# Halo attention and a factored convolution on one core: in layer 0, when the row loads are issued, where the top rows' transfers stand, how the norm's steps are spread, and what is loaded first

## The chip, the core and the metric

The kernel runs on one core of a Trainium2 chip. A core has five engines with an instruction stream each: PE (matrix products), DVE (vector), ACT (scalar functions), POOL and SP, and 16 DMA engines that move data between the memories. In this kernel SP does nothing but issue transfers, in the order in which they are written; one that has to wait holds up all behind it. The metric is the time on the device in microseconds (us), over several runs. Everything is in 32-bit floating point.

## The reference, cut to what matters

The input `x` is two images of 128 channels by 256 by 256.

```python
# layer 0: group norm, attention inside windows of 8 x 8 pixels, residual
x = x + attention(gn(x))
#   q, k, v = W_qkv applied to each pixel; 4 heads of 32
#   a window's 64 queries see the 12 x 12 pixels around it, less those that FIXED_MASK strikes out
#   logits = q k + relative position (row, column) + FIXED_MASK; softmax; times v; W_out
# layer 1: group norm, a vertical convolution of 5 taps and one of 3, times a mix of 8 groups; residual
x = x + conv(gn(x))
```

Group norm needs the mean and the variance of the whole image (4 channels to a group) before any pixel of it can be normalised: `gn` of image 0 stands ahead of all attention. The mask leaves, for each query, 6 x 6 of the 12 x 12 keys, so that even and odd pixel rows fall apart into separate problems.

## The kernel before, in words

Layer 0 is `attention_fast`. Its first part, the setup, loads all of image 0 in 32 pieces of 8 rows (`f_sx`, 1 MB each, L266), and DVE takes their statistics two rows at a time with `bn_stats` (L128). The constants (`f_wqkvT`, `f_hot` and others) are loaded ahead of these pieces by `cload` (L201) and L244, L246. `load_rows(0)` and `load_rows(1)` come last and bring the first two strips for the attention itself.

The attention then goes through 64 strips `k` (32 to an image, 8 new rows each), and each strip in two units `u = 2k` and `u = 2k + 1` (even and odd pixel rows), 128 units in all. All engines' orders, SP's too, are those of the written code (`manual_schedule(engines=ORDERED)`). A unit is, on PE: `biases` (L565), `scores` (L582), the next unit's `keys` (L385, `f_pk`), the next strip's `coefficients` (L476, `f_pa`), `attend` (L608, `f_o`), then in an even unit the next strip's `values` (L498, `f_pv`), in an odd one two units' `queries` (L448, L450), and last `project` (L385, `f_py`). `PIECES` sets into how many matmuls some of these are cut. ACT takes the exponentials (L592), four in a unit, as the scores come; DVE the reciprocals of the softmax's sums (L614), three in a unit.

What SP issues in layer 0, by name:

- `load_rows(k + 2)`, at the start of an even unit: the 10 rows of a later strip into one of three `f_raw` buffers, in five transfers of two rows (L319). DVE normalises them in `normalise(k + 2)` at the start of the odd unit (L359), the first thing that it does there.
- `load_next()`, right after it, in image 0 alone: up to 10 rows of image 1 for its statistics, into the one buffer `f_sx`, also by twos (L306). `input_stats` reads them at the start of the next even unit.
- `bring(r, ...)`: the values from `f_vn` to where the windows need them, `f_vt`, in 6 or 12 transfers (L528, L532, L535), for `r = 0` after `values` of the even unit, for `r = 1` after `attend` of the odd unit, whose reads of `f_vt1` it has to wait for.
- `bring_top(r, b)`: 12 small transfers (L545, L549, L552) of an image's first two rows from `f_top`, a tile that shares the buffer of `f_sx`. `bring_top(1, 0)` stands ahead of unit 0, `bring_top(1, 1)` at the end of unit 63, after that unit's `bring(1, ...)`.
- the store of the unit's result (L646), at the unit's end, waiting for DVE's `project` (L642).

Between the statistics and a usable mean stand six steps (`Norms.steps`): a matmul, a row of short DVE instructions, a matmul, a DVE instruction, a square root on ACT, and DVE again. Unit 60 takes all six for image 1's input, unit 70 all six for image 0's result, at fixed places called `step()`.

Layer 1, `convolutions_fast`, follows at about 1906 us.

## Time and profile before

| | |
|---|---|
| runs, median (lowest to highest) | 2912.95 us (2910.43 to 2917.16) |
| the profiled execution's own time | 2912.66 us |
| its span on the core | 2910.7 us |
| PE busy / DVE / ACT / POOL | 95% / 73% / 52% / 22% of the span |
| granted PE clock, mean | 0.997 |
| setup, until the first unit | 113.2 us |
| units 0 and 1 | 32.8 us |
| units 2 to 59 (image 0) | 814.2 us |
| units 60 to 65 (from image 0 to image 1) | 93.0 us |
| units 66 to 127 (image 1) | 853.2 us |
| the rest (layer 1) | 1004.3 us |

A unit begins with the first matmul of L565, so the lengths of the units are the distances between these in the timeline. In the profile, a row of the waits names the engine and line that waited, what ended the wait, the total, how often, and the longest. A row of the timeline gives start, length, engine, line, operation, tiles, how many such instructions are merged in it, and in brackets the idle time before it and what ended it; "issue" stands where the profile shows nothing that the engine waited for.

### The profile page before, as it was taken

How to read it: one execution, taken by the hardware profiler on the slowest of the kernel's cores; microseconds unless marked ns; L12 is line 12 of the kernel's file. 1: busy time of each engine (PE TensorE's matmuls, PEld its weight loads, DVE VectorE, ACT ScalarE, POOL GpSimd, SP SyncE). 2: the span in 40 equal slices, each digit the busy share in tenths (PEclk: the TensorE clock that was granted, in tenths of full speed). 3: DMA queues.
4: the chain of work that ended last, by engine and by line, in shares of the span. 5: the costliest groups of instructions: out<-in, count | busy, mean ns of one | idle time of the engine just before them, and what ended most of it. 6: DMA issues, size and time to landing. Idle time of an engine off the chain costs nothing.

```text
span 2910.7 us, 117791 instructions
## 1 busy us (share of the span) xinstructions
PE 2766.5 (95%) x51762; PEld 2095.5 (72%) x51762; DVE 2134.0 (73%) x3601; ACT 1506.9 (52%) x2379; POOL 643.1 (22%) x2049
## 2 busy tenths in 40 slices
PE   0699999999999999999999999999999999999998
PEld 0489899899989888999998999954444444444444
DVE  8567667676666656555565665579999998999987
ACT  0345454454545545454544545456666666666654
POOL 1233333333333333333323333200000000000000
PEclk9999999999999999999999999999999999999999
DMA  9666666666666455555555555557888887888885
GB/s 394 208 187 173 189 174 179 181 160 188 175 162 164 125 146 126 138 141 136 140 126 137 138 138 140 129 142 210 221 220 214 216 218 213 222 212 212 221 217 146
DMA packets 207528, 521.89 MB, mean 179 GB/s; under 512 B 26304, under 2 KB 103584, under 8 KB 178336
## 3 DMA queue, kind: packets, MB, share of 16 engines
q1 hardware_dynamic: 197936, 448.19, 53.1%
q0 software_dynamic: 9072, 66.06, 12.2%
q8 instruction: 412, 6.75, 1.0%
q14 instruction: 108, 0.88, 0.1%
HBM read 284.78 MB, written 134.22 MB: 144 GB/s over the span
## 4 chain that ended last, share of the span: by engine, by line
PE 77%; issue 18%; POOL 1%; DVE 1%; SPq 1%; DMA 1%; ACT 1%; POOLq 0%; DVEq 0%; ACTq 0%
PE f_s L582 9%; PE f_o L608 8%; PE f_pk L385 8%; PE f_pv L498 8%; PE f_py L385 8%; PE a_o L890 6%; PE a_e L890 6%; PE f_pq L450 6%; PE f_pa L476 5%; PE f_s L565 5%; PE f_pq L448 2%; PE a_d L941 2%; PE a_c L890 1%; PE b L983 1%; PE g L870 1%
## 5 line engine op out<-in xcount | busy, mean ns | idle before, releaser
L489 DVE TENSOR_SCALAR f_cf<-f_pa,f_keep 128x512 f32<-128x512 f32 x128 | 103.7, 810 | 534.4 <-ACT f_cf L485 534.3
L592 ACT ACTIVATE f_p<-f_s 128x512 f32<-128x512 f32 x512 | 264.4, 602 | 419.9 <-PE f_s L582 419.9
L456 ACT ACTIVATE f_q<-f_pq,f_head 128x512 f32<-128x512 f32 x512 | 303.6, 703 | 150.3 <-PE f_pq L450 150.3
L399 POOL COPY f_kt<-f_kt 128x60 f32<-128x60 f32 (+1 forms) x348 | 106.2, 341 | 1202.4 <-ACT f_kt L413 1178.6
L376 POOL COPY f_xq<-f_xn 128x96 f32<-128x96 f32 x1024 | 337.2, 362 | 9.9 <-DVE f_xn L359 9.9
L965 ACT ACTIVATE t<-t,w 128x1024 f32<-128x1024 f32 x127 | 145.9, 1148 | 368.6 <-DVE t L958 363.7
L972 DVE SCALAR_TENSOR_TENSOR t<-t,w,t 128x1024 f32<-128x1024 f32 x254 | 325.9, 1283 | 7.4 <-ACT t L965 1.3
L582 PEld LDWEIGHTS f_s<-f_q,f_kt 64*64 64x64 f32 x17176 | 270.3, 132 | 49.2 <-issue 49.2
L582 PE MATMUL f_s<-f_q,f_kt 64*64 64x64 f32 (+1 forms) x17176 | 287.8, 220 | 0.0
L608 PE MATMUL f_o<-f_vt,f_p 128*32 128x66 f32 x16384 | 269.6, 220 | 14.2 <-issue 14.1
L608 PEld LDWEIGHTS f_o<-f_vt,f_p 128*32 128x32 f32 x16384 | 244.3, 108 | 27.2 <-issue 18.0
L498 PE MATMUL f_pv<-f_wqkvT,f_xn 128*128 128x128 f32 x2048 | 251.0, 279 | 10.9 <-issue 9.4
L385 PE MATMUL f_pk<-f_xn,f_wqkvT 128*128 128x192 f32 (+3 forms) x1496 | 257.9, 322 | 0.7 <-ACT f_kt L413 0.7
L1001 POOL DMA_DIRECT2D y<-f_x x63 | 54.7, 868 | 918.7 <-DVE y L993 871.3
L498 PEld LDWEIGHTS f_pv<-f_wqkvT,f_xn 128*128 128x128 f32 x2048 | 235.4, 192 | 20.2 <-issue 13.4
L385 PE MATMUL f_py<-f_ot,f_woT 128*128 128x160 f32 (+1 forms) x1520 | 245.9, 311 | 3.0 <-DVE f_ot L626 1.8
L890 PE MATMUL a_o<-xm,w1s 128*128 128x512 f32 x512 | 242.2, 594 | 4.4 <-ACT t L881 4.4
L890 PE MATMUL a_e<-xm,w1s 128*128 128x512 f32 x512 | 240.7, 591 | 0.0
L385 PEld LDWEIGHTS f_py<-f_ot,f_woT 128*128 128x128 f32 x1520 | 228.9, 191 | 5.4 <-issue 2.2
L385 PEld LDWEIGHTS f_pk<-f_xn,f_wqkvT 128*128 128x128 f32 x1496 | 221.4, 190 | 12.6 <-issue 1.7
L450 PE MATMUL f_pq<-f_xn,f_wq_s 128*128 128x192 f32 (+1 forms) x1008 | 210.2, 331 | 0.0
L615 DVE TENSOR_TENSOR f_on<-f_o,f_rc 128x320 f32<-128x320 f32 (+1 forms) x384 | 197.1, 513 | 13.3
(149 smaller groups left out, 4663.2 us busy)
## 6 DMA issues: line engine op xcount, KB each, us to landing
f_raw<-in_x SPq DMA_DIRECT2D x308, 256.0 KB
f_x<-f_x SPq DMA_DIRECT2D x128, 512.0 KB
y<-f_x POOLq DMA_DIRECT2D x63, 1024.0 KB, 7.8
out<-y SPq DMA_DIRECT2D x63, 1024.0 KB
f_vt<-f_vn SPq DMA_DIRECT2D x172, 264.0 KB
raw<-f_x SPq DMA_DIRECT2D x64, 640.0 KB
f_sx<-in_x SPq DMA_DIRECT2D x32, 1024.0 KB
f_sx<-in_x SPq DMA_DIRECT2D x128, 256.0 KB
```

Of the source, the lines that this page charges most:

```text
L376: nc.gpsimd.tensor_copy(xq[:, half, t2, 1:4, :, c].rearrange("p t r n e -> p r t n e"), xn[k % 2][:, windows, :, c, 0:3, t2:8:4].rearrange ...
L385: nc.tensor.matmul(dst[:, 512 * lo // last : 512 * hi // last], w, moving[:, n * lo // last : n * hi // last], start=True, stop=True,)
L450: nc.tensor.matmul(by_pair[:, lo:hi, 8:32], wq_s, xn[k % 2][:, lo:hi, r, c, 0:3].rearrange("p n i j -> p n (i j)"), start=True, stop=True,)
L456: nc.scalar.activation(q[:, c, :, i].rearrange("p n (j t) -> p n j t", t=4), pq.rearrange("p (n t j) -> p n j t", n=NPAIR, t=4), AF.Copy, ...
L498: nc.tensor.matmul(pv[:, P * n : P * n + P], xn[k % 2][:, 4 * g + n].rearrange("p r c i j -> p (r c i j)"), wvT, start=True, stop=True,)
L582: nc.tensor.matmul(sc[g][n // 8][64 * c : 64 * c + 64, n % 8, lo:hi].rearrange("p i x -> p (i x)"), kt[r][rows, c, NKEY * n : NKEY * n + 6 ...
L592: nc.scalar.activation(pts[u][:, g, 8 * half : 8 * half + 8].rearrange("p n i x -> p (n i x)"), sc[g][half].rearrange("p n i x -> p (n i x ...
L608: nc.tensor.matmul(po[32 * h : 32 * h + 32, n - lo], p[:, h // 2, n, h % 2], vt[r][:, :, n, h], start=True, stop=True,)
L615: nc.vector.tensor_tensor(on[:, :, lo:hi].rearrange("p c n d -> p n c d"), po[:, :, :, 0:32], rc.to_broadcast([P, hi - lo, 2, 32]), ALU.mult,)
L890: nc.tensor.matmul(pa[:, : n * W], w, rows, start=i == 0, stop=i == len(terms) - 1)
L965: nc.scalar.activation(t3[:, j : j + 4], t1[:, j : j + 4, :], AF.Copy, scale=w3[:, 0:1])
L972: nc.vector.scalar_tensor_tensor(t3[:, j : j + 4], t1[:, j + tap : j + tap + 4, :], w3[:, tap : tap + 1], t3[:, j : j + 4], ALU.mult, ALU.add,
```

## The change

- `load_rows` is one transfer of 10 rows. It moves from the start of the even unit to after `scores`, and waits for the first exponential of the same unit (`after(...)` adds a dependence on an instruction).
- `load_next` is one transfer too. It moves to after `attend`, and waits for the unit's first reciprocal.
- `bring_top(1, b)` moves behind the `load_rows` of an image's first unit (units 0 and 64).
- The norm's steps go through a queue `chains`: two places in a unit, four in those of strips `NS - 2`. Image 1's input norm starts in unit 59; image 0's result norm starts in unit 70 as before and takes three units.
- In the setup, three pieces of `f_sx` are issued ahead of the constants, the first of them by twos. The pieces begin at row 16; the first 16 rows come with `load_rows(0)` and `load_rows(1)`, which stand at the end of the pieces and serve both the statistics and the attention.

No arithmetic is added or removed.

```diff
+        def load_rows(k, behind=None):
+            b, s = divmod(k, NS)
+            t = rawp.tile([P, 10, W], F32, tag="raw", name=f"f_raw_{k}")
+            n = min(10, H - 8 * s)
+            load = nc.sync.dma_start(t[:, 0:n, :], x[b, :, 8 * s : 8 * s + n, :])
+            if behind:
+                after(load, behind)
+            raws[k] = t
...
+            for i in range(first):
+                t = sp.tile([P, 8, W], F32, tag="sx", name=f"f_sx_0_{i}")
+                for lo in range(0, 8, 8 if i else 2):
+                    hi = lo + (8 if i else 2)
+                    nc.sync.dma_start(t[:, lo:hi], x[0, :, 8 * (i + 2) + lo : 8 * (i + 2) + hi, :])
+                ahead.append(t)
+            for t, src in constants:
+                nc.sync.dma_start(t, src)
...
+            for i in range(first, NS - 2):
+                t = sp.tile([P, 8, W], F32, tag="sx", name=f"f_sx_0_{i}")
+                nc.sync.dma_start(t, x[0, :, 8 * (i + 2) : 8 * (i + 2) + 8, :])
+                statistics(i, t)
+            for i in range(2):
+                load_rows(i)
+                statistics(NS - 2 + i, raws[i][:, 0:8])
...
-            norm_at[2 * (b * NS + NS - 2)] = st_x, b + 1, f"x{b + 1}"
-            norm_at[2 * ((b + 1) * NS + 3)] = st_y, b, f"y{b}"
+            last = 2 * (b * NS + NS - 2)
+            norm_at[last - 1] = st_x, b + 1, f"x{b + 1}"
+            norm_at[last + 10] = st_y, b, f"y{b}"
...
-                for lo in range(0, n, 2):
-                    nc.sync.dma_start(t[:, lo : lo + 2], x[b, :, row + lo : row + lo + 2, :])
+                after(nc.sync.dma_start(sxs[u], x[b, :, row : row + n, :]), seen["output"])
...
-            m = n if k < 2 else 2
-            for lo in range(0, n, m):
-                nc.sync.dma_start(t[:, lo : lo + m], x[b, :, 8 * s + lo : 8 * s + lo + m, :])
...
-                if r == 0:
-                    if k + 2 < NB * NS:
-                        load_rows(k + 2)
-                elif k + 2 < NB * NS:
+                if r == 1 and k + 2 < NB * NS:
                     normalise(k + 2)
...
-                if u == 0 or u in stats_at:
-                    load_next()
...
                 scores(u, pieces(u)[3])
-                step()
+                if r == 0:
+                    if k + 2 < NB * NS:
+                        load_rows(k + 2, seen["exp", 0, 0])
+                    if s == 0:
+                        bring_top(1, b)
                 step()
...
                     emit(keys(u + 1, cuts, cuts))
                 step()
-                step()
...
-                step()
+                if k % NS == NS - 2:
+                    step()
                 attend(u)
+                if u == 0 or u in stats_at:
+                    load_next()
                 if more and r == 1:
                     bring(1, slots_of(k + 1))
-                    if at_top:
-                        bring_top(1, b + 1)
...
                 turn(u)
-                step()
+                if k % NS == NS - 2:
+                    step()
```

## The prediction, made before the changed kernel was run

> **What bounds the kernel now.** I read the page first, then the waits, then the timeline of PE unit by unit. Page and waits:
>
> ```profile
> PE 2766.5 (95%) x51762; PEld 2095.5 (72%) x51762; DVE 2134.0 (73%) x3601; ACT 1506.9 (52%) x2379; POOL 643.1 (22%) x2049
> ...
> q8 instruction: 412, 6.75, 1.0%
> ...
> PE f_o L608 <- issue: 14.1, 23, 1.5
> ...
> DVE f_xn L359 <- DMA f_raw<-in_x: 11.5, 2, 6.2
> ...
> PE f_pv L498 <- issue: 9.4, 17, 1.4
> ```
>
> PE is the bound, and hardly waits for an engine. What it waits for is called "issue": nothing that the profile shows. The timeline of PE says where. Unit 78, and unit 80 with the same work:
>
> ```profile
> 1227.98 0.67 PE L608 MATMUL f_o<-f_vt,f_p 128*32 128x66 f32 x32
> 1229.41 1.59 PE L608 MATMUL f_o<-f_vt,f_p 128*32 128x66 f32 x96 [0.76 <-issue]
> 1230.92 3.84 PE L498 MATMUL f_pv<-f_wqkvT,f_xn 128*128 128x128 f32 x32
> ...
> 1256.33 2.05 PE L608 MATMUL f_o<-f_vt,f_p 128*32 128x66 f32 x128
> 1258.30 3.84 PE L498 MATMUL f_pv<-f_wqkvT,f_xn 128*128 128x128 f32 x32
> ```
>
> Unit 80 takes 13.67 us, unit 78 takes 14.65, and the whole difference is in f_o. From the starts of all units: 59 of the 62 odd ones from 3 to 125 take 13.7 to 13.9, so 13.7 is what PE's work needs. Even units run over it: units 2 to 58 by 19.2 us together (mostly inside f_pv), units 66 to 124 without 70 by 13.3 (nearly all inside f_o). Sum 32.5 us.
>
> Its cause is in the packet records. Queue 8 moves 412 packets of 16,384 bytes; PE has 103,524 matmul and weight-load instructions, 251 to a packet, so these are PE's own program. All long gaps end 1.2 to 1.6 us after such a packet. Three come in a unit. The first of an even unit starts at +4.1 to +4.3 us in units that lose nothing and at +4.9 to +5.5 in those that lose 0.65 to 1.3 in f_o; the second starts at about +8 in image 1, but at +9 to +10 in image 0, where f_pv is late. What holds them is in the same records: the store's 1 KB packets fill the DMA engines from +2.0 to +4.0, the row load's 2 KB packets from +4.0 to +7.6, and in image 0 the load for the statistics makes that +12.5.
>
> Two larger losses stand alone:
>
> ```profile
> 1033.08 0.59 SPq L646 DMA_DIRECT2D f_x<-f_x  x1
> 1033.71 3.07 SPq L319 DMA_DIRECT2D f_raw<-in_x  x5
> ...
> 1043.45 1.92 DVE L359 TENSOR_SCALAR f_xn<-f_raw,mean_x,rstd_x 128x512 f32<-128x512 f32 x4 [5.35 <-DMA f_raw<-in_x]
> ...
> 1046.15 0.69 PE L448 MATMUL f_pq<-f_xn,f_wq_s 128*128 128x128 f32 x2 [3.99 <-DVE f_cf L489]
> ```
>
> Unit 64's row load leaves SP only after unit 65 has begun (1033.06), behind 24 transfers, 12 of them bring_top's; DVE waits for it and PE for DVE. Unit 65 takes 20.2 us; after its gap some query matmuls take 1.49 us where 0.82 is usual (the granted clock of that stretch is 0.97). Unit 1 has the same at its row load (128.3): 17.2 us.
>
> **The change part by part.**
>
> *Row load moved and joined (even units).* Removes four of five issues. The first exponential of a unit ends at +3.0 (1252.56 + 0.60 in unit 80, begun at 1250.14). The row load then issues at +3.05; packets have followed an issue by 1.2 to 1.4 us, so they start at +4.4, after the first program packet's +4.1, where now they are queued right behind the store. Two 10-row loads stand in this trace (the setup's last): 10,240-byte packets of 0.39 us, eight to an engine, 3.1 us; it is over at about +7.5, when the second program packet is due, and lands near +8.5, over 5 us before the odd unit's normalise. Behind the waiting issue SP holds only the statistics load, bring(0) and the store, due at +8, +14 and +18: none is late. POOL issues no transfer in layer 0.
>
> *Statistics load moved.* The first reciprocal ends at +8.1 (unit 16: 352.34 + 0.22 against 344.47), so its packets run from about +9.4 to +12.5, after the second program packet and ahead of bring(0) at +13.9. Its buffer is read 14 us later. The third program packet (+12.4) has until the odd unit's +2.3.
>
> Worth together: at most the 32.5 us. I take 28.5, seven eighths, as the store still holds the first packet at times.
>
> Here a rule speaks against the change. The Trainium skill, "DMA: Bandwidth & Descriptors", section "Queues, rings and completion order": a DMA engine takes turns between queues by whole packets, about 9 to 17 descriptors, before it switches. What the trace counts as packets would be its descriptors, and the eight of a load go in one turn: 0.76 us as it is (8 x 0.095), 3.1 as changed. The delays seen now, 0.8 in image 1, fit it. So if a program packet falls behind the new load, it pays four times as much; the gain rests on the place of the load, not on its form.
>
> Another rule says there is nothing to gain: "Runtime: NRT & Kernel Launch", section "Instruction fetch mechanics", has the program stream in by 16 KiB blocks and the crossing of one mostly hidden. By it this part is worth 0. Unit 78 beside unit 80 says otherwise, 0.98 us in one unit. I go by the row.
>
> *bring_top behind the row load, units 0 and 64.* Unit 64's load leaves about 8 us earlier (12 issues of 0.62 to 0.67), near 1025.6, and lands near 1031, before unit 65 wants it. bring_top's 12 then end near 1034, 5 us before attend(65) (1039.4); unit 63's store, 8 us earlier too, frees DVE's 3.5 us wait. Unit 65 falls from 20.2 to 13.9 or so: 6.2 (between 4 and 6.5, all of its excess). Unit 1 has 3.5 to give. But the statistics load of unit 0 uses bring_top's buffer and waits for its last landing, and can then hold a program packet in unit 1: 2.5 (between 0.5 and 3.5).
>
> *Norm steps.* Unit 70 takes 16.5; f_pk there takes 3.7 us for 1.9 because both steps stand before it and ACT's copies come late. Spread, the two matmuls' 0.5 stay, and the square root brings its two table loads (1.28 us each) right after unit 72's exponentials, with some 1.5 us of slack ahead of f_o. I take 1.8 (between 0 and 2.8), and 0.3 in unit 60.
>
> *Setup.* DVE's statistics run without a gap from the first landing:
>
> ```profile
> 4.49 54.01 SPq L266 DMA_DIRECT2D f_sx<-in_x  x25
> ...
> 9.54 19.90 DVE L128 BATCH_NORM_STATS2 f_st_x<-f_sx 128x6 f32<-128x512 f32 x32 [9.54 <-DMA f_sx<-in_x]
> ```
>
> The first two rows, issued at 1.2, land near 3.9 (f_wqkvT took 2.5): 5.6 us earlier. But the DMA engines are full there (422 GB/s, 2.5 us for 1 MB) and DVE needs 2.45: it starves for 1.9 us ahead of the second piece and 1.5 ahead of the fourth, which the constants (0.55 MB, 1.4 us) delay, and 0.7 is lost on the first piece by twos and at the joins. Two loads fewer do not help DVE, which still takes 128 statistics of 0.61. Worth 1.4 (between 0 and 3).
>
> Sum against the profiled execution: 28.5 + 6.2 + 2.5 + 1.8 + 0.3 + 1.4 = 40.7. 2912.7 - 40.7 = 2872.0; that execution is within 0.3 us of the median of the runs. Layer 1's orders are not touched.
>
> **The rivals.**
>
> *Only the single losses go.* PE's program packets stay late, behind the store and the values' transfers (SBUF packets of 0.8 us), and the gaps move but stay. For it: the first packet has only 0.05 to 0.2 us to spare even in good units (+4.3, and f_o is hit from about +4.35). Against: good units have the store in front too. 2912.7 - 12.2 = 2900.5.
>
> *A program packet falls behind the joined load.* Slower. In two of three even units the first program packet starts at +4.1 or later, and the load's packets come at +4.4. If the load gets in first, the packet waits up to 3.1 us more and f_o with it. There are 62 loads, some 41 in such units: 41 x 3.1 = 127 more. With the 12.2 of the rest, 2912.7 + 127 - 12 = 3028 at worst, about 2945 where it hits a third of them. It decides from the point where 13 units (40.7 / 3.1) are hit. Against it: the exponential sets the load by PE's own progress, so the distance holds from unit to unit.
>
> *Nothing happens:* the waits of PE have another cause and the two late loads become other waits (unit 65 now for bring_top, unit 1 for the statistics load). 2910 to 2915.
>
> **How the numbers follow.** All parts as summed: 0.68, time 2872, own range 2860 to 2887. Only the single losses, or these with up to half of the gaps: 0.15, 2887 to 2904. Slower by the joined load: 0.11. Nothing: 0.06, partly on either side. What can be told from no change is 0.2%, 5.8 us. Faster 0.84, within it 0.05, slower 0.11. The range runs from 2859 to 2903, which leaves out the slow cases and little else.
>
> **What would show it.** In the profile after: even units at 13.7 to 13.9 in the timeline; the rows "PE f_o L608 <- issue" and "PE f_pv L498 <- issue" of 14.1 and 9.4 down to a few us; "DVE f_xn <- DMA f_raw" (11.5) nearly gone; units 65 and 1 near 14; unit 70 near 14; DVE's first statistics at about 4 us and its last some 1.4 us earlier than 91.1; program packets at +4.1 and +8. Wrong if f_o or f_pv rows with "issue" gaps of 2 to 3 us appear (the joined load got in front), if bring_top shows up as what attend(65) waits for, or if f_xn waits for f_raw in every odd unit.

## The result, and the profile after

The changed kernel takes 2878.03 us (median of 4 runs, 2876.19 to 2879.55), beside 2914.32 us for the kernel before on the same chip (2910.43 to 2917.16). The ratio is 0.9876, with a 95% interval from 0.9859 to 0.9893: it is 1.2% faster. The forecast was 2872.0 with a range from 2859 to 2903. The profiled execution has a span of 2875.9 us, 34.8 less than before.

The page of the changed kernel, the lines of PE and of the queue that carries its program:

```profile
PE 2753.5 (96%) x51762; PEld 2090.1 (73%) x51762; DVE 2134.2 (74%) x3601; ACT 1506.2 (52%) x2379; POOL 640.4 (22%) x2049
...
q8 instruction: 412, 6.75, 0.9%
```

The instructions and the program packets are the same in number. The waits of PE in the changed kernel (engine, line, what ended the wait: total us, times, longest), where L634 is now `attend` and L524 `values`:

```profile
PE f_pq L474 <- issue: 4.9, 1, 4.9
...
PE f_o L634 <- issue: 3.4, 3, 1.7
...
PE f_pv L524 <- issue: 0.3, 1, 0.3
```

The two rows that stood at 14.1 and 9.4 us are down to 3.4 and 0.3. The row of `f_pq` is now the largest inside the units, one wait of 4.9 us. Before, it was one wait too, and in unit 1 as well:

```profile
PE f_pq L448 <- issue: 1.9, 1, 1.9
...
142.51 0.38 PE L448 MATMUL f_pq<-f_xn,f_wq_s 128*128 128x128 f32 x1 [1.88 <-issue]
```

Unit 78 in the timeline of PE, which had lost 0.98 us in `f_o`, and the first line of unit 79:

```profile
1201.53 1.12 PE L591 MATMUL f_s<-f_cf,f_hot 32*64 32x256 f32 x32
...
1207.73 2.05 PE L634 MATMUL f_o<-f_vt,f_p 128*32 128x66 f32 x128
1209.70 3.84 PE L524 MATMUL f_pv<-f_wqkvT,f_xn 128*128 128x128 f32 x32
...
1215.21 1.12 PE L591 MATMUL f_s<-f_cf,f_hot 32*64 32x256 f32 x32
```

`f_o` is in one piece, and the unit takes 13.68 us. Unit by unit, from the first matmul of `biases` in each:

| stretch | before | after | difference | predicted |
|---|---|---|---|---|
| setup, until unit 0 | 113.2 | 115.1 | +1.9 | -1.4 |
| unit 0 | 15.6 | 15.8 | +0.2 | 0 |
| unit 1 | 17.2 | 21.0 | +3.8 | -2.5 |
| even units 2 to 58, over 13.7 each | 19.2 | 0.2 | -19.0 | } |
| even units 66 to 124 without 70 and 72, over 13.7 each | 13.3 | -0.1 | -13.4 | } -28.5 |
| unit 65 | 20.2 | 14.0 | -6.2 | -6.2 |
| units 70 and 72 | 30.2 | 29.8 | -0.4 | -1.8 |
| all else (unit 126 -1.4, layer 1 -0.5, unit 60 -0.1) | | | -1.7 | -0.3 |

In all -34.8. "Layer 1" begins here, as in the table before, with the first matmul of unit 127, whose work runs into that of layer 1 (so "units 66 to 127" there are units 66 to 126). Unit 126 and layer 1 differ as much between two executions of one kernel: layer 1 took 1003.8 us in this profile of the changed kernel and 1006.3 in a second one, unit 126 12.9 and 15.2.

The program packets, from the packet records: the first of an even unit now starts at +4.1 us (median; latest +4.4 in all 59 units), where in units 66 to 124 before 16 of 30 had started later than +4.4. The second starts at +8.0 in image 0 (before +9.3) and at +8.1 in image 1 (before +8.7).

Unit 65, on SP's queue, on DVE and on PE. SP's queue:

```profile
1012.89 0.57 SPq L253 DMA_DIRECT2D f_raw<-in_x  x1
1013.51 0.94 SPq L571 DMA_DIRECT2D f_vt<-f_top  x1
...
1017.92 0.62 SPq L571 DMA_DIRECT2D f_vt<-f_top  x1
1021.63 0.63 SPq L575 DMA_DIRECT2D f_vt<-f_top  x1
```

DVE:

```profile
1020.67 1.29 DVE L670 TENSOR_TENSOR f_x<-f_py,f_raw 128x512 f32<-128x512 f32 x2
1021.88 1.92 DVE L385 TENSOR_SCALAR f_xn<-f_raw,mean_x,rstd_x 128x512 f32<-128x512 f32 x4
```

The row load leaves SP in the middle of unit 64 (which began at 1005.67), ahead of the twelve transfers of `bring_top`, and DVE normalises right after its own work, with no wait for the load. The 5.35 us of DVE and the 3.99 of PE are gone.

Unit 1 went the other way. SP's queue, and PE:

```profile
122.32 0.39 SPq L253 DMA_DIRECT2D f_raw<-in_x  x1
...
127.67 0.62 SPq L571 DMA_DIRECT2D f_vt<-f_top  x1
131.75 0.63 SPq L575 DMA_DIRECT2D f_vt<-f_top  x1
...
134.41 0.61 SPq L578 DMA_DIRECT2D f_vt<-f_top  x1
136.67 0.33 SPq L342 DMA_DIRECT2D f_sx<-in_x  x1
```

```profile
140.97 0.27 PE L474 MATMUL f_pq<-f_xn,f_wq_s 128*128 128x128 f32 x1
146.10 0.58 PE L474 MATMUL f_pq<-f_xn,f_wq_s 128*128 128x128 f32 x1 [4.86 <-issue]
146.48 1.49 PE L476 MATMUL f_pq<-f_xn,f_wq_s 128*128 128x384 f32 x2
```

Unit 0's statistics load (L342) uses the buffer out of which `bring_top` reads, and leaves SP only at 136.67, when unit 1 (from 130.99) is 5.7 us old. Its packets run from 137.6 on, `bring`'s are right behind them, and the next program packet starts at 143.3. PE stands for 4.86 us until it has come, and its next matmuls take 1.49 us for 0.81: the granted clock is 0.50 for 6.83 us from 144.06 on.

### The profile page after: what moved, and what is told of

Read it like the earlier page. It is cut to its first block, busy times and chain, and to the rows that moved or that the text cites. A ratio compares the mean times of both kernels' runs of the same rounds, so it can differ in the third digit from the quotient of the medians.

```text
span 2875.9 us, 117447 instructions
## 1 busy us (share of the span) xinstructions
PE 2753.5 (96%) x51762; PEld 2090.1 (73%) x51762; DVE 2134.2 (74%) x3601; ACT 1506.2 (52%) x2379; POOL 640.4 (22%) x2049
## 3 DMA queue, kind: packets, MB, share of 16 engines
q0 software_dynamic: 9072, 66.06, 12.3%
## 4 chain that ended last, share of the span: by engine, by line
PE 79%; issue 17%; POOL 1%; DMA 1%; ACT 1%; DVE 1%; SPq 0%; POOLq 0%; ACTq 0%; DVEq 0%
PE f_s L608 10%; PE f_o L634 9%; PE f_pk L411 8%; PE f_pv L524 8%; PE f_py L411 8%; PE a_o L919 6%; PE a_e L919 6%; PE f_pq L476 6%; PE f_pa L502 5%; PE f_s L591 5%; PE f_pq L474 2%; PE a_d L970 2%; PE a_c L919 1%; PE b L1012 1%; PE g L899 1%
## 5 line engine op out<-in xcount | busy, mean ns | idle before, releaser
L634 PE MATMUL f_o<-f_vt,f_p 128*32 128x66 f32 x16384 | 263.6, 220 | 3.4 <-issue 3.4
L634 PEld LDWEIGHTS f_o<-f_vt,f_p 128*32 128x32 f32 x16384 | 241.8, 108 | 12.9 <-issue 2.0
L524 PE MATMUL f_pv<-f_wqkvT,f_xn 128*128 128x128 f32 x2048 | 246.0, 279 | 0.6 <-DVE f_cf L515 0.3
L524 PEld LDWEIGHTS f_pv<-f_wqkvT,f_xn 128*128 128x128 f32 x2048 | 233.7, 192 | 6.7 <-DVE f_cf L515 0.5
L411 PEld LDWEIGHTS f_pk<-f_xn,f_wqkvT 128*128 128x128 f32 x1496 | 221.5, 190 | 12.5 <-issue 1.7
L643 DVE TENSOR_TENSOR f_on<-f_o,f_rc 128x320 f32<-128x320 f32 (+1 forms) x384 | 197.2, 514 | 13.3
```

What stands on the lines that cost most here:

```text
L411: nc.tensor.matmul(dst[:, 512 * lo // last : 512 * hi // last], w, moving[:, n * lo // last : n * hi // last], start=True, stop=True,)
L524: nc.tensor.matmul(pv[:, P * n : P * n + P], xn[k % 2][:, 4 * g + n].rearrange("p r c i j -> p (r c i j)"), wvT, start=True, stop=True,)
L634: nc.tensor.matmul(po[32 * h : 32 * h + 32, n - lo], p[:, h // 2, n, h % 2], vt[r][:, :, n, h], start=True, stop=True,)
L643: nc.vector.tensor_tensor(on[:, :, lo:hi].rearrange("p c n d -> p n c d"), po[:, :, :, 0:32], rc.to_broadcast([P, hi - lo, 2, 32]), ALU.mult,)
```

## The experiments

Each was timed beside the kernel before on its chip; that kernel's median was between 2915.7 and 2920.2 us in these sets. Lengths of stretches are from the profiled execution of each. This table is the frame for what follows:

| kernel | ratio to before (95%) | setup | units 0, 1 | even 2 to 58 over 13.7 | even 66 to 124 over 13.7 (without 70, 72) | unit 65 |
|---|---|---|---|---|---|---|
| before | 1 | 113.2 | 15.6, 17.2 | 19.2 | 13.3 | 20.2 |
| after | 0.9876 (0.9859 to 0.9893) | 115.1 | 15.8, 21.0 | 0.2 | -0.1 | 14.0 |
| e1 place only | 0.9881 (0.9862 to 0.9901) | 113.7 | 15.9, 15.9 | 6.6 | 0.1 | 14.1 |
| e2 form only | 1.0046 (1.0032 to 1.0060) | 113.1 | 15.6, 17.9 | 34.1 | 14.6 | 20.0 |
| e3 no wait | 1.0025 (1.0016 to 1.0033) | 115.2 | 15.8, 19.9 | 38.6 | 10.3 | 13.7 |
| e4 old setup | 0.9848 (0.9829 to 0.9868) | 113.7 | 16.1, 17.8 | 1.1 | -0.4 | 14.0 |
| e5 statistics behind rows | 0.9996 (0.9987 to 1.0005) | 114.9 | 15.6, 16.9 | 38.5 | -0.4 | 14.6 |
| e7 unit 1 | 0.9867 (0.9846 to 0.9889) | 115.0 | 16.1, 18.1 | 1.0 | -0.4 | 14.0 |
| e8 before, shifted | 1.0794 (1.0766 to 1.0821) | 112.5 | 14.4, 16.4 | 89.9 | 101.7 | 18.2 |
| e9 after, shifted | 1.0938 (1.0890 to 1.0986) | 114.3 | 14.4, 14.5 | 128.0 | 111.5 | 15.1 |
| b1 | 0.9854 (0.9828 to 0.9879) | 113.7 | 16.1, 13.6 | 5.0 | -0.2 | 14.0 |
| b2 | 0.9856 (0.9833 to 0.9880) | 114.3 | 15.9, 13.9 | 4.3 | -0.3 | 14.0 |
| b3 | 0.9862 (0.9845 to 0.9878) | 112.8 | 15.9, 16.4 | 1.3 | 0.6 | 14.3 |

### Place, form and wait of the two loads (e1, e2, e3)

The change does three things to the two loads at once: it puts them later among SP's issues, makes one transfer of five, and lets them wait. The first run keeps place and wait and takes the form back:

```diff
-            load = nc.sync.dma_start(t[:, 0:n, :], x[b, :, 8 * s : 8 * s + n, :])
-            if behind:
-                after(load, behind)
+            m = 2 if behind else n
+            for lo in range(0, n, m):
+                load = nc.sync.dma_start(t[:, lo : lo + m], x[b, :, 8 * s + lo : 8 * s + lo + m, :])
+                if behind and lo == 0:
+                    after(load, behind)
...
-                after(nc.sync.dma_start(sxs[u], x[b, :, row : row + n, :]), seen["output"])
+                for lo in range(0, n, 2):
+                    load = nc.sync.dma_start(t[:, lo : lo + 2], x[b, :, row + lo : row + lo + 2, :])
+                    if lo == 0:
+                        after(load, seen["output"])
```

> The changed kernel with its row loads and statistics loads cut into pieces of two rows again; they stay where the change put them, the first piece behind the exponential or the reciprocal. Theory 'place' (the gain comes from the load's packets coming after the program packet): the same gain, 2875 to 2884 us, even units at 13.7 to 13.8. Theory 'form' (few large packets are handled better, or fewer issues of SP count): most of the 31 us in the even units is lost, 2900 to 2912. Theory 'size of a turn' (a packet of 2 KB yields sooner than one of 10 KB): a little faster than the changed kernel, by up to 5 us, most of it in unit 1.

Measured: 2884.38 us, ratio 0.9881, just above the range that I had expected of "place". Image 1 has the whole gain with the old form (0.1 us over). Image 0 has two thirds of it (6.6 over, and odd units 4.1 over, where the changed kernel has 0.8). PE's waits, with `values` at L529:

```profile
PE f_pv L529 <- issue: 3.7, 9, 0.7
```

The row load in pieces is over later (its last packet ends at +9.3 in the median of image 1, where nothing follows it, instead of +8.7), and the second program packet comes at +8.9 (median) instead of +8.0 in image 0 and +8.1 in image 1. It is as late in image 1, where this costs nothing. What differs is the place where PE needs the packet. Before the change PE stops in `f_pv` after 24 to 29 of its 32 matmuls in image 0, and in `f_o` after 31 to 37 of its 128 in image 1. Units 6 and 50 stop in both, 127 matmuls apart; by that distance the second place lies at the end of `f_pv` or behind it in image 1, where the packet is needed later. This is read from the traces and was not tested. In six odd units of image 0 the third packet of the unit before starts only after they have begun, and these make most of the 4.1. Unit 1 loses less here, 15.9 for 21.0, which pays half of that back. Place and wait make the gain; the form is worth some 10 us in image 0 beside it.

The second run has the form alone, in the kernel before:

```diff
-                for lo in range(0, n, 2):
-                    nc.sync.dma_start(t[:, lo : lo + 2], x[b, :, row + lo : row + lo + 2, :])
+                nc.sync.dma_start(sxs[u], x[b, :, row : row + n, :])
...
-            m = n if k < 2 else 2
-            for lo in range(0, n, m):
-                nc.sync.dma_start(t[:, lo : lo + m], x[b, :, 8 * s + lo : 8 * s + lo + m, :])
+            nc.sync.dma_start(t[:, 0:n, :], x[b, :, 8 * s : 8 * s + n, :])
```

> The kernel before with its row loads and statistics loads each joined to one transfer, at the old place and behind nothing. Theory 'place', with the rule of turns by whole packets: a program packet that falls behind a joined load waits up to 3.1 us instead of 0.76, in about 40 of the 62 even units, so up to 90 us slower, 2945 to 3010. Theory 'form': about as fast as the changed kernel in the even units, 2880 to 2890. If joining matters neither way: 2908 to 2918.

Measured: 2931.46 us, ratio 1.0046, between the ranges that I had expected. PE's waits in that kernel, with `values` at L495 and `attend` at L605:

```profile
PE f_pv L495 <- issue: 26.1, 28, 1.6
PE f_o L605 <- issue: 21.8, 22, 4.6
```

So the joined load at the old place is a loss, but one of 15 us in image 0 (34.1 for 19.2) and 1.3 in image 1, not of 90. The longest single wait of 4.6 is one case. In image 1, where the row load stands alone, as many first program packets are late as before (16 of 30 after +4.4), and the latest starts at +5.7, before +5.5. The charge of 3.1 us for a packet behind a joined load, which was estimated from the rule of turns, is not seen: image 0's second packet comes at +10.1 (before +9.3).

The third run leaves the changed kernel as it is but for the two waits:

```diff
             load = nc.sync.dma_start(t[:, 0:n, :], x[b, :, 8 * s : 8 * s + n, :])
-            if behind:
-                after(load, behind)
...
-                after(nc.sync.dma_start(sxs[u], x[b, :, row : row + n, :]), seen["output"])
+                nc.sync.dma_start(sxs[u], x[b, :, row : row + n, :])
```

> The changed kernel without its two waits: both loads stay one transfer and stay where they are written among SP's issues, but nothing holds them until the exponential or the reciprocal. Theory 'place': the row load then issues right behind the store, as before, and its packets come ahead of the first program packet; the gain of the even units is gone, 2905 or slower (slower still by the rule of turns, to 2990). If the order of SP's issues alone does it: 2875 to 2885.

Measured: 2926.64 us, ratio 1.0025. PE's waits, with `values` at L522 and `attend` at L632:

```profile
PE f_pv L522 <- issue: 27.5, 27, 1.7
PE f_o L632 <- issue: 15.8, 19, 2.3
```

The even units lose 38.6 and 10.3 us, about as with the joined form at the old place (34.1 and 14.6), and of the large gains only unit 65's stays (13.7). SP runs ahead of the unit: without the wait it issues the row load at +1.6 (median) instead of +3.0, and the statistics load at +3.4 instead of +8.1. The place in the written order decides little without the wait.

### Each load for itself (e5)

The statistics load, right behind the row load, with no wait of its own (that of unit 0 stays as it is; `u` in the first part is the unit that reads the load, 2 for unit 0's):

```diff
-                after(nc.sync.dma_start(sxs[u], x[b, :, row : row + n, :]), seen["output"])
+                load = nc.sync.dma_start(sxs[u], x[b, :, row : row + n, :])
+                if u == 2:
+                    after(load, seen["output"])
...
                 if r == 0:
                     if k + 2 < NB * NS:
                         load_rows(k + 2, seen["exp", 0, 0])
+                    if u in stats_at:
+                        load_next()
...
-                if u == 0 or u in stats_at:
+                if u == 0:
                     load_next()
```

> The changed kernel, but the statistics loads of units 2 to 58 are issued right behind the unit's row load and wait for nothing of their own (unit 0's still waits for the reciprocal). Theory 'place, for each load': their packets now run from about +7.5 to +10.6 us of the unit, on top of the second program packet (due at +8), which then comes at about +10, as in the kernel before with joined loads; f_pv in units 2 to 58 loses some 1 us each, 20 to 30 us in all, 2898 to 2908, and units 66 to 126, which have no such load, stay as in the changed kernel. If the row load's wait alone made the gain: 2876 to 2882.

Measured: 2914.41 us, ratio 0.9996. PE's waits, with `values` at L526:

```profile
PE f_pv L526 <- issue: 32.9, 28, 1.8
```

Image 1 keeps its gain (-0.4). Image 0 is 38.5 us over, 32.9 of it in the waits of `f_pv`: the second program packet comes at +10.2. These 38.5 are 8.5 above the upper end of what I expected (20 to 30), and the time is above its range: the second packet is now late in nearly every unit (28 waits), where `f_pv` had 17 before. So the row load's wait by itself is worth the 13.4 us of image 1, and in image 0 it takes both waits to win the 19.0.

### Is it the program? A shift by half a packet (e8, e9)

Thirty-two more matmuls in the setup, on data that are there, in time in which PE idles. Their results are overwritten by the same values, and nothing else is touched. The profile counts 64 more PE matmuls and 64 more weight loads: 128 instructions, half of the 251 of a packet.

```diff
-                nc.tensor.matmul(
-                    pg[:, : 2 * NREL], wq_nat[32 * h : 32 * h + 32, :],
-                    relT[32 * h : 32 * h + 32, :], start=True, stop=True,
-                )
+                for _ in range(9):
+                    nc.tensor.matmul(
+                        pg[:, : 2 * NREL], wq_nat[32 * h : 32 * h + 32, :],
+                        relT[32 * h : 32 * h + 32, :], start=True, stop=True,
+                    )
```

> The kernel before with 32 extra matmuls in the setup (in time that PE is idle), 128 PE instructions, half of a program packet; all else is untouched. If the gaps of the even units are PE's program coming late, they must leave their places: the three crossings of a unit lie about 2.3 us earlier (near +0, +4.4 and +9.3 instead of +2.3, +6.6 and +11.6), so f_o and the end of f_pv no longer show gaps and other lines do; the sum can be larger or smaller, 2900 to 2940. If the gaps belong to the lines or to an engine's late result: same rows f_o and f_pv 'issue', 2912 to 2922.

> The changed kernel with the same 32 extra matmuls. The new places of the loads were read against where the program packets stand now. If the gain depends on that: the packets come about 2.3 us earlier in the unit, into the store's transfer (+2 to +4) and into the row load (+4.4 to +7.5), and the even units lose again, 2890 to 2930. If any spacing of the loads does it: 2876 to 2884.

Measured: 3147.45 us for the kernel before with the shift, 1.0794 of the kernel before, and 3199.1 us for the changed kernel with the shift, 1.0938. Both are far outside all that I had expected. PE's waits in the kernel before with the shift (`attend` at L609):

```profile
PE f_o L609 <- issue: 182.2, 110, 4.3
```

And its unit 80 in the timeline of PE:

```profile
1394.83 1.62 PE L609 MATMUL f_o<-f_vt,f_p 128*32 128x66 f32 x97
1398.96 0.66 PE L609 MATMUL f_o<-f_vt,f_p 128*32 128x66 f32 x31 [2.50 <-issue]
1399.56 5.47 PE L499 MATMUL f_pv<-f_wqkvT,f_xn 128*128 128x128 f32 x32
```

The waits of `f_pv` are gone, and `f_o` stops instead, 110 times in the 128 units and up to 4.3 us, in unit 80 after 97 of its 128 matmuls (`f_pk` stops 28 times, for 17.0 us). How far the stop has moved can be read in unit 78, which before stopped after 32 matmuls of `f_o`:

```profile
1361.98 1.59 PE L609 MATMUL f_o<-f_vt,f_p 128*32 128x66 f32 x96
1365.81 1.11 PE L609 MATMUL f_o<-f_vt,f_p 128*32 128x66 f32 x32 [2.25 <-issue]
```

The stop stands 64 matmuls with their 64 weight loads away from there, as many instructions as were added; the same holds in units 66, 110 and 122 (after 31, 36 and 37 before, after 95, 100 and 101 here). Packet records of unit 80: program packets at +1.9, +7.9 and +12.3; the row load's packets start at +3.7 and nine tenths of them are over by +7.4, the last at +10.4. PE goes on at +10.3, 1.4 us after the second packet has come (7.93 + 0.93). In the odd units, which have no row load, the second packet starts at +6.2 (median of image 1). Against these, the even ones have it 1.7 us later (median +7.87 for +6.18) with the row load in pieces of 2 KB, and 1.95 us later (+8.15 for +6.20) as one transfer of 10-KB packets in the changed kernel with the shift. After such a gap the values can be slower too: 5.47 us for 3.84. The changed kernel with the shift has the same row, larger:

```profile
PE f_o L635 <- issue: 214.7, 111, 6.8
```

128 instructions that no engine waits for move the time by 231 us in one kernel and by 321 in the other. Of the 231, from unit 0 to unit 127, 168 are idle time of PE (204 us for 36) and 62 are slower matmuls; the granted clock stands at 0.50 in 23 stretches of 3.41 us there. Nothing but the place of the program's blocks has changed, against the transfers and against the matmuls. That settles what PE waits for under the name "issue". What makes a packet late is not settled as far: the odd units, in which neither of the two loads runs, lose 64 us too with the shift (35.2 in image 0 and 28.3 in image 1), and what delays their packets was not looked into. The pair also says that the change is good for one alignment: with the shift the changed kernel is the slower of the two by 1.6% (3199.1 against 3147.45, same chip).

### The setup (e4, and the late constants in b2)

The changed kernel with the setup of before:

```diff
-            for i, t in enumerate(ahead):
-                statistics(i, t)
-            for i in range(first, NS - 2):
...
-            for i in range(2):
-                load_rows(i)
-                statistics(NS - 2 + i, raws[i][:, 0:8])
+            for s in range(NS):
+                t = sp.tile([P, 8, W], F32, tag="sx", name=f"f_sx_0_{s}")
+                nc.sync.dma_start(t, x[0, :, 8 * s : 8 * s + 8, :])
+                norm.chunk(st_x[0], 4 * s, t)
...
+            load_rows(0)
+            load_rows(1)
```

> The changed kernel with the setup of the kernel before (constants first, the statistics' loads in the old order, the two row loads behind them). By the traces the changed setup ends 1.9 us later than the old one, so this should be faster than the changed kernel by about 1.9 us: 2875 to 2877, with unit 0 starting near 113.2 us. If what follows the setup gives it back (the program packets stand otherwise, unit 1 meets its load otherwise): within 1 us of the changed kernel.

Measured: 2875.9 us, ratio 0.9848, whose interval overlaps that of the changed kernel. Unit 0 begins at 113.7 (115.1 in the changed kernel; 114.9 to 115.3 in four more profiles of that setup, 113.7 in e1's), and unit 1 takes 17.8 for 21.0. Two other stretches give some of it back (unit 126 takes 13.9 us, layer 1 1004.8).

Why the new setup is later is in DVE's timeline of the changed kernel:

```profile
4.16 0.69 DVE L128 BATCH_NORM_STATS2 f_st_x<-f_sx 128x6 f32<-128x512 f32 x1 [4.16 <-DMA f_sx<-in_x]
...
10.40 5.04 DVE L128 BATCH_NORM_STATS2 f_st_x<-f_sx 128x6 f32<-128x512 f32 x8 [1.94 <-DMA f_sx<-in_x]
17.67 12.42 DVE L128 BATCH_NORM_STATS2 f_st_x<-f_sx 128x6 f32<-128x512 f32 x20 [2.24 <-DMA f_sx<-in_x]
...
91.81 1.02 DVE L136 BATCH_NORM_AGGREGATE mv_x<-f_st_x 128x2 f32<-128x192 f32 x1
```

Before, that last row was:

```profile
90.04 1.02 DVE L136 BATCH_NORM_AGGREGATE mv_x<-f_st_x 128x2 f32<-128x192 f32 x1
```

DVE begins 5.4 us earlier (4.16 for 9.54), but then waits: 0.33, 0.28 and 0.91 within the first piece, 1.94 before the second, 2.24 before the fourth, 0.25 later, 0.20 and 0.63 before the two row loads, whose ten rows come slower than DVE takes eight of them. That is 6.8 us of waits, and the last aggregate begins 1.8 us later. The constants stood between the third and the fourth piece; as SP issues `f_wq_nat`, `f_relT` and the fourth piece only at 7.76, 10.39 and 12.96, I took SP's waits for the cause and put the constants behind the sixth piece. This was done in one kernel with the edits of the next part:

```diff
-            first = 3
+            first = 6
```

> The same, but with the changed setup, its seven constants issued behind the sixth piece of the input instead of behind the third. Theory 'SP waits for the eighth transfer before': the two waits of VectorE ahead of the second and the fourth piece (1.94 and 2.24 us in the changed kernel) shrink to below 1 us each, the last aggregate moves from 91.8 to between 88.5 and 90, unit 0 begins at 111.5 to 113.5. Theory 'every byte of the constants costs VectorE the same wherever it stands': the last aggregate stays at 91 to 92. In all 2866 to 2870 by the first, 2869 to 2872 by the second.

DVE in that kernel:

```profile
10.43 12.46 DVE L128 BATCH_NORM_STATS2 f_st_x<-f_sx 128x6 f32<-128x512 f32 x20 [1.79 <-DMA f_sx<-in_x]
25.32 4.98 DVE L128 BATCH_NORM_STATS2 f_st_x<-f_sx 128x6 f32<-128x512 f32 x8 [2.44 <-DMA f_sx<-in_x]
...
91.82 1.02 DVE L136 BATCH_NORM_AGGREGATE mv_x<-f_st_x 128x2 f32<-128x192 f32 x1
```

The wait of 2.24 us has moved with the constants to the seventh piece, as one of 2.44, and the last aggregate is where it was, at 91.82. My theory of SP's waits falls: the constants cost DVE 2.2 to 2.4 us at both places. It seems that DVE, with 12.4 us for five pieces, hardly gets ahead of the loads; that reason is argued and was not tested. The time of this kernel, 2876.19 us, is above both ranges, by about what unit 2 loses in the next part.

### Unit 1, and the norm's first step (e7, b1, b2, b3)

If the statistics load of unit 0 held the program packet, then unit 1 must recover when that load comes at another time. First attempt: strip 2's rows loaded right behind the setup, and the first `bring_top` back ahead of unit 0.

```diff
+        load_rows(2)
         weights.load()
...
+            bring_top(1, 0)
             by_place(0, (0, 4))
...
-                    if k + 2 < NB * NS:
+                    if 0 < k < NB * NS - 2:
                         load_rows(k + 2, seen["exp", 0, 0])
-                    if s == 0:
+                    if k == NS:
                         bring_top(1, b)
```

> The changed kernel with strip 2's rows loaded right behind the setup (its buffer is free there), so that unit 0 issues no row load, and with the first bring_top back ahead of unit 0. Unit 0's statistics load then no longer waits for bring_top. Theory 'the statistics load held unit 1's program packet': unit 1 falls from 21.0 to 13.7 to 14.5 us, units 0 and 1 together from 36.9 to 29 to 30, the kernel by about 7 us against the changed one. If unit 1's loss has another cause (the clock, the prologue's transfers): unit 1 stays above 16.5.

Measured: 2879.08 us, ratio 0.9867; unit 1 at 18.1 us, above the 16.5 of the rival. But the load had not moved enough to decide it: SP is still busy with `bring`'s transfers for strip 0, `bring_top`'s packets end near 131.3, and the statistics load runs from 133.1 to 138.4, 2.0 to 7.4 us into unit 1. The program packet starts at 137.95, when the load is nearly over, and `f_o` waits 3.06 us. So it decides nothing; what its trace shows is the same picture with a shorter hold.

Second attempt, on the old setup: the first statistics load is issued in unit 1, behind its first reciprocal. In the same kernel image 0's output norm begins one unit later, which is for unit 70.

```diff
+        load_rows(2)
         weights.load()
...
-                    if k + 2 < NB * NS:
+                    if 0 < k < NB * NS - 2:
                         load_rows(k + 2, seen["exp", 0, 0])
...
-                if u == 0 or u in stats_at:
+                if u == 1 or u in stats_at:
                     load_next()
...
-            norm_at[last + 10] = st_y, b, f"y{b}"
+            norm_at[last + 11] = st_y, b, f"y{b}"
```

> The changed kernel with the setup of the kernel before, strip 2's rows loaded behind the setup, the first statistics load issued in unit 1 behind its first reciprocal instead of in unit 0, and image 0's output normalisation begun in unit 71 instead of 70. Theory 'the statistics load held unit 1's program packet': with it out of the way unit 1 goes to 13.7 to 14.5 us (from 21.0). Rival 'bring_top and the prologue's values hold it': above 16.5. Theory 'the one matmul of the norm in unit 70 makes its keys wait': unit 70 goes to 13.7 and unit 71 up by 0.5 to 2; if the waits belong to unit 70's own shapes: unit 70 stays above 15. In all, if both go well: 7 + 1.5 + 1.5 us under the changed kernel, about 2868.

Measured: 2875.65 us, ratio 0.9854, where I had expected about 2868. Unit 1 takes 13.6 us (13.9 in b2): the load was the cause. But unit 2 takes 18.1 (17.8 in b2). In b2's timeline of PE:

```profile
145.06 1.43 PE L608 MATMUL f_s<-f_q,f_kt 64*64 64x32 f32 x75
148.78 1.77 PE L608 MATMUL f_s<-f_q,f_kt 64*64 64x64 f32 x55 [2.28 <-issue]
```

The load has pushed `bring`'s transfers of unit 1 back, and these hold the next program packet until 146.3, 2.3 us into unit 2. The third attempt puts the load behind unit 1's first exponential instead (`load_next` now takes the instruction that it waits for):

```diff
+                if u == 1:
+                    load_next(seen["exp", 0, 0])
...
-                if u == 1 or u in stats_at:
-                    load_next()
+                if u in stats_at:
+                    load_next(seen["output"])
```

> The kernel with the old setup and the moved first statistics load (b1), that load now behind unit 1's first exponential instead of its first reciprocal: its packets run some 3.5 us earlier in unit 1, in the place that an odd unit has free and an even one gives to the row load, and bring's packets behind them end before the unit does. Theory 'the loss of unit 2 (18.1 us in b1) is the same late program packet, held by what that load pushed back': unit 2 goes to 13.7 to 14.3, unit 1 stays at 13.6 to 14.3, and the kernel is about 4 us under b1, near 2871, 0.983 to 0.985 of the kernel before. If something else makes unit 2 late: it stays above 16 and the time at 2874 to 2877.

Measured: 2872.81 us, ratio 0.9862. Unit 2 is at 13.7, as expected; unit 1 is back at 16.4:

```profile
138.66 0.27 PE L459 MATMUL f_pq<-f_xn,f_wq_s 128*128 128x128 f32 x1
141.47 0.38 PE L459 MATMUL f_pq<-f_xn,f_wq_s 128*128 128x128 f32 x1 [2.53 <-issue]
```

Unit 0's store is late there, behind `bring`; the load follows it with packets from +6.2 to +10.4 of the unit, and the program packet starts at +10.3. At four places of this one load unit 1 or 2 took 7.3, 4.4, 4.4 and 2.7 us more than 13.7, in the changed kernel, e7, b1 and b3: the loss goes where the load goes, and I found no place free of it. The sizes are not to be compared closely, as with the load at the changed kernel's place unit 1 took 21.0 there, but 20.4 in its second profile, 17.8 in e4 and 16.9 in e5.

Unit 70 is settled by b1, b2 and b3: 13.7 us in all three, for 15.7 in the changed kernel, with units 71 to 74 at 55.7 for 55.5 (b2 against the changed kernel), so the 0.5 to 2 us that I had expected unit 71 to lose did not come. The changed kernel's timeline of PE in unit 70:

```profile
1094.40 1.13 PE L411 MATMUL f_pk<-f_xn,f_wqkvT 128*128 128x256 f32 x4 [0.74 <-ACT f_kt L439]
1096.32 1.15 PE L502 MATMUL f_pa<-f_xq,f_wb 128*64 128x64 f32 x32 [0.78 <-ACT f_kt L439]
```

Before, two waits of 0.74 us for ACT's copies stood there as well, one at `f_pk` and one at the norm's second matmul:

```profile
1114.16 1.13 PE L385 MATMUL f_pk<-f_xn,f_wqkvT 128*128 128x256 f32 x4 [0.74 <-ACT f_kt L413]
1116.03 0.38 PE L161 MATMUL pv_y<-q_y,f_gavg 128*128 128x1 f32 x2 [0.74 <-ACT f_kt L413]
```

The change took that matmul away, and `f_pa` waits in its stead. The first matmul of the norm alone makes both waits, and with it out of the unit they are gone. Why one matmul more ahead of the keys makes them wait for the copies was not found out.

b1, b2 and b3 beat the changed kernel only in the sum of these stretches: unit 127 begins at 1868.0, 1867.5 and 1864.9 us in them. For the changed kernel it is 1872.1, and 1875.1 in a second set:

> The changed kernel as it is, beside the two others on one chip: 0.986 to 0.989 of the kernel before.

That set, beside b1 and b2, gave 2877.59 us for the changed kernel, ratio 0.9859 (0.9836 to 0.9881). The intervals of all of them overlap: their gain of some 4 to 10 us in layer 0 is in the profiles, and not established in the times.

## Why the prediction was right, and where not

The time was in the range and 6.0 us above the forecast. Some 5 us too little had been counted for the gaps and for what was left out, and some 11 too much for unit 1, the setup and the norm's steps. That these errors partly cancel is luck.

- *What bounds the kernel.* Right. PE waits for its own program, whose packets are late behind data; the shift shows it by moving the waits to other instructions, and e1 to e5 that the two loads are the data. Two readings of the packets were too rough: units that lost nothing had their first packet at +3.1 to +4.3 and not +4.1 to +4.3, and the second stood at +8.7 (median) in image 1 and not at about +8. The rule of the Trainium skill ("Runtime: NRT & Kernel Launch", "Instruction fetch mechanics") that a crossing is mostly hidden holds here only where the packet is on time, as it is after the change in nearly all of the 59 even units. Where it is not, one crossing cost up to 1.5 us in `f_o` before, 4.86 us in unit 1 after, and 2.5 us in the shifted unit 80. A reckoning by that rule alone, with nothing to gain here, was 32 us off.
- *Row load and statistics load moved, 28.5.* Right in mechanism, and undersized: 32.4 measured. The eighth that I kept back, "as the store still holds the first packet at times", did not occur; the first packet starts by +4.4 in every even unit. The issues came when the step said, at +3.04 and +8.12 (medians; said +3.05 and +8.1), and the packets nearly: row packets from +4.0 to +8, the last to +8.7 (said +4.4 to +7.5), statistics from +9.3 to +13 (said +9.4 to +12.5). One thing failed without harm. The row load was to start behind the first program packet, but its packets follow the issue by 1.0 us and not by 1.2 to 1.4; in 32 of the 56 even units with a 10-row load they start ahead of it, by up to 0.4 us. By the prediction's second rival 13 such units would have used up the gain. None of the 32 was late on that account, and the program packet started by +4.4 in all; why that little lead did no harm was not tested, and to that extent the gain was luck.
- *The weighing of "DMA: Bandwidth & Descriptors", "Queues, rings and completion order".* The row in the trace and the rule gave the same 0.8 us for pieces, and so I took the 3.1 estimated from the rule for the joined load. Measured on the second packet of image 1 with the shift, the hold is 1.7 us with pieces and 1.95 with the joined load, which there starts 0.3 later: it does not grow by four with the size of what one transfer gives an engine. The direction was right (joined at the old place: 0.46% slower), the price was not. The conclusion that the gain rests on the place held.
- *Unit 65, 6.2.* Right, to the tenth.
- *Unit 1, 2.5.* Wrong: +3.8. The step named what happened ("can then hold a program packet in unit 1") and priced it too low, with a gain of at least 0.5. It failed in the time of `bring_top`'s last landing: the eighth of its twelve issues waits until the row load, eight transfers back, has landed (issued at 131.75), so the statistics load left 5.7 us into unit 1, and one program packet was held behind that load and `bring` together, for 4.86 us. It is what the rival "a program packet falls behind the joined load" said of the row loads, here of one statistics load. Of the 3.5 us that unit 1 had to give, 1.88 were such a wait already, which the prediction had put down to the row load.
- *Norm steps, 1.8 and 0.3.* 0.4 and 0.1. The failed step is "f_pk there takes 3.7 us for 1.9 because both steps stand before it": the first one alone suffices. With it moved out (b2), unit 70 and the four behind it gain 1.85 us against the changed kernel.
- *Setup, 1.4.* Wrong: +1.9. The waits that were named came (1.9 predicted and 1.94 measured before the second piece), but those within the first piece came to 1.5 us, where 0.7 had been allowed for these and the joins together, the constants cost 2.24 and not 1.5, and the joins with the row loads 0.83 more. That makes 6.8 us of waits, where 4.1 had been summed, against an earlier start of 5.4.

The rival "only the single losses go" was wrong in its one claim: the store ahead of the first packet did not hold it. The rival "nothing happens" named rightly that unit 1's late load turns into a loss through the statistics load.

## What to carry to other kernels

When a busy PE shows gaps that end at "issue", look for its program's packets among the DMA records and compare their start with the units that lose nothing: a transfer of several microseconds should not run when the next packet is due, and a wait on an instruction of the unit (here the first exponential, the first reciprocal) is what holds it off, since SP's order alone does not. Such a fit belongs to one alignment of the program; any edit that adds PE instructions ahead of the loop can cost more than the tuning won, so the packets have to be looked at again after it. A load that has to be moved takes its delay along: ask what is queued behind it at the new place, and which packet that will hold.

## What was not expected of the hardware

- 128 PE instructions more, in idle time, made the kernel before 7.9% slower and the changed one 9.4% (3147.45 and 3199.1 us). In the kernel before, the waits grew from 23.5 us in `f_o` and `f_pv` to 199.2 in `f_o` and `f_pk`.
- With the shift, a program packet that comes due during a 10-row load started when most of the load was over, in both forms: +7.9 with 2-KB packets and +8.1 with 10-KB packets, where +6.2 is usual in the units without a load.
- SP's ninth issue waited for the landing of the first, twice in the rows above: the row load at 122.32 and at 1012.89, seven issues at their usual distance, and the eighth after it only at 131.75 and at 1021.63, 0.02 us after the row load's last signal in both places. In the changed kernel's trace all 1849 transfers of SP signal their landing on eight semaphores in strict turn, so the ninth takes that of the first. The wait may well be the program's and not the chip's; no run tells these apart.
- After a wait for the program, PE's next matmuls could run at half pace: 1.49 us for 0.81 in unit 1 after 4.86 us, 5.47 for 3.84 in the shifted unit 80 after 2.50 us. After the 2.53 us in b3 they did not. The granted clock says it: 0.50 for 6.83 us from 144.06 in the first case, for 3.41 us from 1399.89 in the second, and 1.00 at that place in b3. The 0.97 that the prediction gives for unit 65 is a mean as well; there the clock was 0.50 for 3.41 us. In all 14 traces the units have 78 such stretches, of 3.41 or 6.83 us, and in the 3.41 us ahead of each PE was busy for at most 46%.
